# A DiT block on one core: attention output in one block per unit, and beats dealt anew

## The chip, the cores and the metric

The kernel runs on one core of a Trainium2 chip. The time is the device time of one execution in microseconds, the median of several executions. A profiled execution gives, beside its own time, the span from the first to the last instruction and what each engine did in it: TensorE (PE for matmuls, PEld for weight loads), VectorE (DVE), ScalarE (ACT), GpSimd (POOL) and SyncE (SP), which issues nearly all DMAs.

## The reference

A PixArt-style transformer block over 16 sequences of 256 tokens of width 256, in 16 heads of 16, in fp32:

```python
c_proj = silu(c) @ W_mod + b_mod                  # six vectors per sequence
q, k, v = split((ln(x) * (1 + scale_a) + shift_a) @ W_qkv + b_qkv)
x = x + gate_a * (softmax(q k^T * 16**-0.5) v @ W_proj + b_proj)
q_c = ln(x) @ W_qc + b_qc;  k_c, v_c = split(ln(context) @ W_kvc + b_kvc)
x = x + softmax(q_c k_c^T * 16**-0.5) v_c @ W_cproj + b_cproj
x = x + gate_m * (gelu((ln(x) * (1 + scale_m) + shift_m) @ W_mlp1 + b_mlp1) @ W_mlp2 + b_mlp2)
```

## The kernel before

**Units.** The work is cut into 32 attention units: a self-attention unit s and a cross-attention unit c for each of the 16 sequences, in the order s0 to s4, then s5 c0 s6 c1 and so on to s15 c10, then c11 to c15 (line 785 on). A set-up ahead of them splits the first weights and makes the first queries and keys; after them comes the MLP, four chunks of the hidden layer for each sequence, whose first pieces are worked in the last units.

**Precision.** A product of two fp32 operands is three passes in fp32r: each operand is cut in a high and a low part (`cut`, `high`, `low`), and high x high, high x low and low x high are added in PSUM.

**Softmax.** For each unit, scores S are first made with queries in rows, only for the row maxima: `s_tile` (line 691) does two matmuls into `s` and one VectorE `tensor_reduce` into `mx`. The maxima are transposed (`m_halves`, `psm`), negated by ScalarE (`m_send`, line 728) and sent by DMA into a spare row of the queries. Then the scores are made again with keys in rows, now less the maximum: `t_part` (line 734) writes `st`. One ScalarE activation, `exp` (line 745), takes both halves of `st` (one for each half of the array) to a `pt` tile: pair k of heads. `st` and `s` have one buffer each in PSUM. `av_part` (line 768) multiplies `pt` with V, which has a column of ones for the sums, into `o`; its matmuls use four groups of 32 columns of the array, where nearly all others use two groups of 64 rows. ScalarE copies `o` to `oT`; it is transposed (A0, A1 in the plan), divided by the sums on VectorE (`norm`, n0, n1), transposed back (`aT`, word a), cut, and projected (P). `end` copies the projection out of PSUM, `add` gates and adds it to x (line 657).

**Beats.** Each unit has eight beats (`beat`, line 1080). In beat k of unit n run: the scores t of pair k of unit n, the maxima's scores s of unit n+1, the projections Q and V of unit n+2 and K of unit n+3, the transposes T and U of normalized context or x for n+3, and the output of units n-1 and n-2. What runs where is written out by hand in `PLAN` (line 1068): each beat has words done ahead, words of an x lane, words of a y lane, and words done after. The lanes are the two row halves of the array: x does rows 0 to 63, y rows 64 to 127; `beside` (line 475) issues from the lane that is behind, counting one for a matmul and 0.53 for a small transpose. "Q12" is twelve matmuls of Q; s and t are two matmuls each. A y-lane piece that continues an accumulation, or the second half of a transpose, has to wait for the end of its x-lane piece (`after`, line 335). The whole plan of before stands as the removed lines at the end of the diff below: one line a beat, and in it the words ahead, the x lane, the y lane, and the words after.

E is the exponential of the beat. o0 is the attention output of pairs 0 to 3 of the unit itself, after beat 4; o1 that of pairs 4 to 7 of the unit before, after beat 0. kh and kl make the high and low part of K (ScalarE, VectorE), qh and ql those of Q; kH, kL, qH, qL send them by DMA. pe is `end`. Te, Ue, ae are ScalarE copies of transposes out of PSUM, Tc, Uc, ac their cuts on GpSimd. Words c, s, e, L are pieces of layer norms (sums on VectorE, the rest on GpSimd, or ScalarE for those called late).

**Order.** Every engine, and SP, runs its instructions in the order in which this program issues them (`InOrder`, line 40, and `ON`). So a wait at the head of an engine's queue holds all behind it.

**Buffers.** PSUM has two banks for `st`, two for `s`, and rings of two for the tags `gen` (Q, V, K, P in the order of their first matmul) and `tr` (transposes, maxima, `o`). In SBUF, `pt` has 5 buffers, `x` 5, `c` (context) 2, `t1` 2, `x1` 7.

**Last stage.** `TW` in `E_` (line 55) says after which beat the MLP's weights are loaded (u), their high parts made (h) and their low parts (l; d means VectorE, else GpSimd).

Of the kernel before, what the change touches and what calls it, by code (L numbers as in the profile page):

```python
# [10 lines left out]
F32 = mybir.dt.float32  # L11
F32R = mybir.dt.float32r
# [9 lines left out]
def pixart_block(  # L22
# [32 lines left out]
    E_ = {'M': (7, 9, 13, 15), 'CUT': 8, 'LN': {'s': 'pool', 'c': 'pool', 'q': 'pool'}, 'ON': (1, 1, 1), 'L0': -16, 'L1': 1, 'S0': -7, 'A0': 0, 'T0': 1, 'S1': 5, 'A1': 7, 'L2': 9, 'T1': 9, 'S2': 32, 'AP': 23, 'DV': (0, 1), 'HP': (1, 0), 'BZ': {}, 'AV': {1: [(1, 2), (1, 3)], 9: [(0, 0), (0, 1)]}, 'AHEAD': (0, 0, 0, 0, 0, 2), 'TW': {(21, 6): 'cb', (23, 6): 'u1', (25, 1): 'u0', (25, 7): 'u2', (27, 1): 'u3', (27, 4): 'h2p', (27, 5): 'h3p', (28, 0): 'l2d', (28, 3): 'u5 h1p', (28, 4): 'h0p', (29, 0): 'l3', (29, 1): 'l0', (29, 3): 'l1d', (29, 6): 'u7', (29, 7): 'u4 u6 h4p', (30, 1): 'h5p h6d', (30, 7): 'l6', (31, 0): 'h7p', (31, 1): 'l4', (31, 2): 'l5', (31, 6): 'l7'}, 'XP': 1, 'IL': 1, 'MF': 0, 'SH': 4, 'RAMP': 1, 'HA': 1, 'MP': 16, 'W': (7, 1, 0, 0), 'PRE': 'z0qp z0kp load rest ld2 one0 silu b12 brow L0a turn L0b b4 L0d scale T0t sc1 hik lok L1a T0h L1b T0l b4 shift hiq K0a L1d bk loq K0m K0h K0x0 K0x1 K0y0p K0y1p T1t K0l T1h K0l0 K0l1 bq T1l Q0a Q0m Q0h Q0x0 Q0y0p Q0x1 Q0y1p Q0l Q0l0 Q0l1 z1kp z1qp K1a K1b hiv lov Q1a Q1b K1x0 K1x1 K1y0 K1y1 K1l K1l0 K1l1 Q1x0 Q1x1 Q1y0 Q1y1 Q1l Q1l0 Q1l1 L2a L2b L2c V0a V0b bv b9 ld3', 'SL': {(-1, 0): 'V1a', (-1, 1): 'T2t T2h T2p vone z2kp z2qp', (-1, 2): 'V1b', (-1, 3): 'rest wm', (-1, 4): 'M0 rest one1 ld4', (-1, 5): 'K2a L3a', (-1, 6): 'K2m L3b L3p L3c', (-1, 7): 'mods sc2 one2 rest', (0, 0): 'gm rest', (0, 1): 'rest', (0, 4): 'rest', (0, 6): 'rest', (1, 0): 'rest', (1, 5): 'rest'}}  # L55
# [35 lines left out]
    ones = const.tile([8, N], F32, name="ones")  # L91
# [18 lines left out]
    def stage(w_ap, c0, name, tag="pt", bufs=5, t=None, q=SP):  # L110
# [49 lines left out]
    ts = [work.tile([P, 2, KC, H], F32, tag="pt", name=f"wf{i}", bufs=5) for i in range(3)]  # L160
# [3 lines left out]
    def f_load():  # L164
        X[0] = work.tile([P, NT, H], F32, tag="x", name="x_0", bufs=5)
# [45 lines left out]
    def setup_rest():  # L211
        gb = work.tile([B, 2, 2, H], F32, tag="pt", name="gb", bufs=5)
        gA, bb = gb[:, 0], gb[:, 1]
        bc = const.tile([1, H], F32, name="bc")
# [25 lines left out]
        wkc, wqc = stage(W_kvc, 0, "wkc_f", "g", 3), stage(W_qc, 0, "wqc_f", "c", 2)  # L240
# [242 lines left out]
    def to_stack(W, src, bias, dst, which, name):  # L483
# [51 lines left out]
        o.high, o.low = high, low  # L535
# [28 lines left out]
    def load(u):  # L564
        if u.kind == "s":
            load_x(u.b)
        elif u.kind == "m":
            mlp_load(u.b)
        else:
            u.ct = work.tile([P, NT, H], F32, tag="c", name=f"c_{u.b}")  # L570
            SP.dma_start(u.ct, tok(ctxt, u.b))
# [28 lines left out]
    def build_post(u):  # L600
# [51 lines left out]
        def end():  # L652
            t1 = work.tile([P, NT, H], F32, tag="t1", name=f"t1_{name}")
            o.t1 = t1
            ACT.copy(t1.rearrange("p t h -> p (t h)"), o.ps)

        def add():
            t1 = o.t1
            if u.kind == "s":
                POOL.tensor_tensor(t1, t1, bc_t(G[b][:, 0]), ALU.mult)  # L660
                X1[b] = o.xg
                POOL.tensor_tensor(X1[b], o.xg, t1, ALU.add)
            else:
                POOL.tensor_tensor(t1, t1, X1[b], ALU.add)
                o.out = t1
# [5 lines left out]
        def finish():  # L671
            o.out = work.tile([P, NT, H], F32, tag="t1", name=f"t1_{name}")
# [72 lines left out]
    def exp(u, pair, st):  # L745
        u.pt[pair] = work.tile([P, 2, NT, N], F32, tag="pt", name=f"pt_{u.n}_{pair}", bufs=5)
# [56 lines left out]
    def mlp_load(b):  # L803
# [3 lines left out]
        m.xt = work.tile([P, NT, H], F32, tag="x" if b > 1 else "c", name=f"x2_{b}", bufs=5 if b > 1 else 2)  # L807
# [55 lines left out]
    def to_hidden(b, c, src, park):  # L863
# [12 lines left out]
        o.high = o.keep = keep  # L876
        o.low = o.send_high = o.send_low = lambda: None
# [11 lines left out]
    def mlp_gelu(b, c):  # L889
        ph = M[b].h.pop(c)  # L890
        homes = (("pt", 5), ("qkh", 3), ("qkl", 3))
        if b == 0 and c:
            homes = (("x1", 7),) + (homes[1:] if c < 3 else (("xTh", 5), ("xTl", 5)))
# [12 lines left out]
    def mlp_second(b, c):  # L906
# [7 lines left out]
        if c == NCH - 1:  # L914
            t1 = work.tile([P, NT, H], F32, tag="t1", name=f"mt_{b}")
# [11 lines left out]
    def tail_word(w):  # L927
# [5 lines left out]
        if c == "u":  # L933
            if j < 4:
                wf[j] = stage(W_mlp1, j * H, f"w1_{j}", "x")
            else:
                wf[j] = work.tile([P, 2, H], F32, tag="x", name=f"w2_{j}", bufs=5)
# [116 lines left out]
    def visit(n, k, home=sp):  # L1054
# [25 lines left out]
    def beat(n, k):  # L1080
# [14 lines left out]
        ls = q4 if q4 and q4.kind in ("s", "m") and q4.ln else None  # L1095
        lx = q3 if q3 and q3.kind == "c" else None
        late = lx and lx.b in (0, B - 2, B - 1)
        early = lc if lc and lc.b not in (0, B - 2, B - 1) else None
# [3 lines left out]
        def attention(v, hf):  # L1102
# [7 lines left out]
            "E": exps, "o1": lambda: attention(prev, 1), "o0": lambda: attention(cur, 0),  # L1110
            "kh": on(q2, lambda: q2.K.high()), "kl": on(q2, lambda: q2.K.low()),
            "kH": on(q2, lambda: q2.K.send_high()), "kL": on(q2, lambda: q2.K.send_low()),
            "qh": on(q2 and hasattr(q2, "Q"), lambda: q2.Q.high()), "ql": on(q2 and hasattr(q2, "Q"), lambda: q2.Q.low()),
# [6 lines left out]
            "n1": on(p1, lambda: p1.norm(1)), "n0": lambda: cur.post.norm(0),  # L1120
            "pe": on(p2, lambda: p2.end()), "hadd": on(p2 and (p2.n == nu - 3), lambda: (p2.add(), p2.store())),
            "add": on(p3, lambda: p3.add()), "gate": on(p1, lambda: p1.gate()),
            "store": on(p3, lambda: p3.store()), "begin": lambda: cur.post.begin(),
            "ld": on(ls and n > 0, lambda: load(ls)),
            "lc": on(c5 and c5.kind == "c", lambda: load(c5)),
            "c1": on(lc, lambda: lc.ln[0].steps[0]()),
            "c2": on(lc or ls and ls.kind == "m", lambda: [f() for f in lc.ln[0].steps[1:]] if lc else mlp_bias(ls.b)),
            "s1": on(ls, lambda: ls.ln[0].steps[0]()),
            "s6": on(ls, lambda: ls.ln[0].steps[1]()),
            "s7": on(ls, lambda: ls.ln[0].steps[2]()),  # L1130
            "e5": on(early, lambda: early.ln[1].steps[0]()),
            "e6": on(early, lambda: [f() for f in early.ln[1].steps[1:]]),
# [7 lines left out]
            "A1": on(p1, lambda: p1.halves(1)), "A0": lambda: cur.post.halves(0),  # L1140
# [149 lines left out]
```

## Time and profile before

| | us |
|---|---|
| median of 3 runs | 747.91 (747.2 to 749.27) |
| the profiled execution's own time | 746.75 |
| its span, first to last instruction | 745.0 |
| the 32 units, from about 33 us on | some 525 |
| the MLP behind them, from about 558 us | some 187 |

In the views below, a group of instructions is named out<-in by the program's names: `mx<-s` is the reduction of the scores for the maxima, `pt<-st` the exponential. In a list in order of time, the first two columns are the start and the length in us, and xN is a run of N instructions merged; in a list of groups, the last columns are busy us, the mean of one in ns, and idle time of the engine ahead of them with what ended it.

### The profile page before, as it was taken

The numbers are of one execution on the slowest core, as the hardware profiler recorded it, in microseconds if no ns is written. First come the engines' busy times: TensorE is split into PE (matmuls) and PEld (weight loads), VectorE is DVE, ScalarE is ACT, GpSimd is POOL, SyncE is SP. The second block draws the span as 40 slices with busy tenths as digits, with TensorE's granted clock in tenths as the row PEclk, the third lists the DMA queues.
The fourth block names the chain that finished last, engine by engine and source line by source line (L and its number), as shares of the span: only waits on it lengthen the run. The fifth ranks groups of instructions, "written<-read, shape, count | busy, mean of one in ns | idle before, by whom it ended". The sixth has DMA issues, their size and how long they took to land.

```text
span 745.0 us, 25353 instructions
## 1 busy us (share of the span) xinstructions
PE 734.8 (99%) x10144; PEld 648.7 (87%) x10144; DVE 578.8 (78%) x1190; ACT 564.2 (76%) x978; POOL 490.1 (66%) x610
## 2 busy tenths in 40 slices
PE   9999999999999999999999999999999999999997
PEld 8778888888888888888888888878878999999997
DVE  4888898988888888888889888898726656666662
ACT  4278888888888888888888888888895666666663
POOL 6756676857667485765758678667566666666553
PEclk9999999999999999999999999999999999999999
DMA  6755445443644544454444545544213132221211
GB/s 207 200 147 153 133 126 143 123 130 100 171 120 128 146 117 145 109 165 128 136 142 123 158 129 160 153 115 126 70 59 100 49 80 70 61 85 43 85 45 43
DMA packets 78809, 87.98 MB, mean 118 GB/s; under 512 B 8610, under 2 KB 64196, under 8 KB 78692
## 3 DMA queue, kind: packets, MB, share of 16 engines
q1 hardware_dynamic: 78356, 85.58, 40.4%
q8 instruction: 80, 1.31, 0.8%
q0 software_dynamic: 192, 0.52, 0.3%
q10 hardware_dynamic: 144, 0.26, 0.2%
q14 instruction: 37, 0.30, 0.1%
HBM read 26.97 MB, written 8.46 MB: 48 GB/s over the span
## 4 chain that ended last, share of the span: by engine, by line
PE 95%; DVE 2%; issue 1%; POOL 1%; ACT 1%; POOLq 0%; DVEq 0%; ACTq 0%
PE s L51 18%; PE st L51 16%; PE o L51 16%; PE ph L51 11%; PE ps_qc L51 5%; PE ps_q L51 4%; PE ps_kc L51 3%; PE ps_P_s L51 3%; PE ps_v_s L51 3%; PE ps_v_c L51 3%; PE ps_k L51 3%; PE ps_P_c L51 2%; PE ps_h L51 1%; PE psT_q L51 1%; PE psA_c L51 1%; PE psT_m L51 1%
## 5 line engine op out<-in xcount | busy, mean ns | idle before, releaser
L51 DVE TENSOR_REDUCE mx<-s 128x2 f32<-128x512 f32 x504 | 324.8, 684 | 63.1 <-PE s L51 56.5
L51 ACT ACTIVATE pt<-st 128x1024 f32<-128x1024 f32 x252 | 258.8, 1027 | 17.7 <-PE st L51 11.7
L51 PE MATMUL s<-big 63*128 63x256 f32 (+1 forms) x1024 | 184.6, 298 | 0.5 <-DVE mx L51 0.4
L51 PEld LDWEIGHTS s<-big 63*128 63x128 f32 (+1 forms) x1024 | 133.8, 186 | 19.9 <-DVE l_kc L51 6.6
L51 PE MATMUL st<-big 64*128 64x256 f32 (+1 forms) x1024 | 134.3, 298 | 0.3 <-ACT pt L51 0.2
L51 POOL TENSOR_TENSOR hl<-hf,hh 128x512 fp32r<-128x512 f32 x64 | 84.0, 1315 | 66.2 <-ACT hh L51 66.2
L51 PE MATMUL o<-pt,v 128*32 128x256 f32 x2048 | 123.8, 382 | 0.0
L51 PEld LDWEIGHTS st<-big 64*128 64x128 f32 (+1 forms) x1024 | 96.1, 185 | 16.2 <-issue 12.9
L51 PEld LDWEIGHTS o<-pt,v 128*32 128x32 f32 x2048 | 60.0, 109 | 41.4
L51 ACT ACTIVATE hf<-ph,bT 128x256 f32<-128x256 f32 x114 | 47.8, 472 | 26.8 <-PE ph L51 26.8
L51 ACT ACTIVATE hh<-ph,bT 128x256 fp32r<-128x256 f32 x114 | 47.8, 471 | 24.2 <-PE st L51 12.8
L51 ACT COPY oT<-o 128x512 f32<-128x512 f32 x63 | 36.9, 585 | 32.8 <-PE o L51 32.8
L51 DVE TENSOR_SCALAR xn_m<-x,mv_m,rs_m 128x256 f32<-128x256 f32 x28 | 26.1, 973 | 38.0 <-POOL rs_m L51 38.0
L51 PE MATMUL s<-big,hh 128*128 128x256 f32 x256 | 46.8, 282 | 0.0
L51 PE MATMUL st<-big,hh 128*128 128x256 f32 x256 | 46.5, 281 | 0.0
L51 PE MATMUL ph<-wkch,wself 128*128 128x256 f32 x224 | 45.0, 284 | 0.0
L51 PE MATMUL ph<-wqch,wself 128*128 128x256 f32 x224 | 44.9, 284 | 0.0
L51 PE MATMUL ps_k<-xTh_s,wself 64*128 64x256 f32 (+1 forms) x232 | 43.8, 294 | 0.0
L51 PE MATMUL ps_q<-xTh_s,wself 64*128 64x256 f32 (+1 forms) x240 | 39.7, 283 | 0.4 <-DVE l_q L51 0.4
L51 PE MATMUL ps_v_s<-wself,xTh_s 64*128 64x256 f32 x224 | 39.2, 294 | 0.0
L51 PE MATMUL ps_P_s<-wself,xTh_as 64*128 64x256 f32 x256 | 39.0, 282 | 0.0
L51 PEld LDWEIGHTS st<-big,hh 128*128 128x128 f32 x256 | 39.0, 188 | 0.0
(245 smaller groups left out, 2469.2 us busy)
## 6 DMA issues: line engine op xcount, KB each, us to landing
big<-h_kc SPq DMA_DIRECT2D x64, 128.0 KB
big<-h_qc SPq DMA_DIRECT2D x64, 128.0 KB
big<-h_k SPq DMA_DIRECT2D x62, 128.0 KB
big<-h_q SPq DMA_DIRECT2D x62, 128.0 KB
big<-l_k SPq DMA_DIRECT2D x32, 128.0 KB
big<-l_q SPq DMA_DIRECT2D x32, 128.0 KB
g<-gd SPq DMA_DIRECT2D x16, 256.0 KB
c<-in_ctx_dram SPq DMA_DIRECT2D x16, 256.0 KB
```

Source lines behind the costliest of these rows:

```text
L51: i = f(*a, **k)
```

## The change

- Both halves of the attention output, o0 and o1, now run for the unit before, one right after the other after beat 0; `E` stands between them on ScalarE. For that `pt` gets 8 buffers. The last unit still does its first half itself (words oz, Az, nz).
- To make room: `x` has 3 buffers and holds the context too (tag `c` is gone), `t1` has one; x is not kept for the residual but loaded a second time, in `begin`, into the `x1` tile where `gate` adds to it. Loads of unit n+5 (`lc`) are all in beat 5. The MLP's inputs go to `xTh` and `xTl`, some weights to `g`, `pt` and `x`, and `TW` is dealt anew, with every cut on GpSimd.
- `end` is VectorE's, not ScalarE's: it multiplies the projection by the gate (s) or adds x (c) on its way out of PSUM; GpSimd's `add` is left with one addition for s, none for c.
- Queries: ScalarE takes both rows blocks out of PSUM with the bias in fp32 (`rows`), and GpSimd makes the high part and the low part (`cut`); before, ScalarE made the high part and VectorE the low part.
- The plan of beats is new. Only the cross units of the first and the last sequence do the layer norm of x late (before: the first and the last two).

```diff
+        def rows():
+            o.hi = work.tile([P, KC, N], F32R, tag="qkh", name=f"h_{name}", bufs=3)
+            o.lo = work.tile([P, KC, N], F32R, tag="qkl", name=f"l_{name}", bufs=3)
+            for f in range(KC):
+                ACT.activation(o.lo[:, f].bitcast(F32), o.ps[:, f * N:(f + 1) * N], AF.Identity, bias=bias[f])
+
+        def cut():
+            POOL.tensor_copy(o.hi, o.lo.bitcast(F32))
+            POOL.tensor_tensor(o.lo, o.lo.bitcast(F32), o.hi, ALU.subtract)
...
+            o.xg = work.tile([P, NT, H], F32, tag="x1", name=f"xg_{b}", bufs=7)
+            SP.dma_start(o.xg, tok(x, b))
 
         def gate():
             if u.kind == "c":
                 return
-            o.xg = work.tile([P, NT, H], F32, tag="x1", name=f"xg_{b}", bufs=7)
-            POOL.tensor_tensor(o.xg, X[b], bc_t(G[b][:, 1]), ALU.add)
+            POOL.tensor_tensor(o.xg, o.xg, bc_t(G[b][:, 1]), ALU.add)
...
         def end():
-            t1 = work.tile([P, NT, H], F32, tag="t1", name=f"t1_{name}")
-            o.t1 = t1
-            ACT.copy(t1.rearrange("p t h -> p (t h)"), o.ps)
+            t1 = work.tile([P, NT, H], F32, tag="t1", name=f"t1_{name}", bufs=1)
+            o.t1 = o.out = t1
+            ps = o.ps.rearrange("p (t h) -> p t h", t=NT)
+            if u.kind == "s":
+                DVE.tensor_tensor(t1, ps, bc_t(G[b][:, 0]), ALU.mult)
+            else:
+                DVE.tensor_tensor(t1, ps, X1[b], ALU.add)
 
         def add():
-            t1 = o.t1
             if u.kind == "s":
-                POOL.tensor_tensor(t1, t1, bc_t(G[b][:, 0]), ALU.mult)
                 X1[b] = o.xg
-                POOL.tensor_tensor(X1[b], o.xg, t1, ALU.add)
-            else:
-                POOL.tensor_tensor(t1, t1, X1[b], ALU.add)
-                o.out = t1
+                POOL.tensor_tensor(X1[b], o.xg, o.t1, ALU.add)
...
-        u.pt[pair] = work.tile([P, 2, NT, N], F32, tag="pt", name=f"pt_{u.n}_{pair}", bufs=5)
+        u.pt[pair] = work.tile([P, 2, NT, N], F32, tag="pt", name=f"pt_{u.n}_{pair}", bufs=8)
...
     PLAN = [
-        ("kh", "s t m1", "m1 t s", "m1s kH E o1 add gate kl"),
-        ("c1", "s t Q12", "t P2 s P10", "L1 ld kL E"),
-        ("", "s t T pe A1 V3", "s t Q4 T A1 Q1", "hadd E L2 Te Tc c2"),
-        ("", "s t V9", "Q1 t s Q6", "E n1"),
-        ("qh store", "s t", "s t qH", "E L3 o0 ql qL"),
-        ("", "t s a E m0 K6", "t s V4 a m0 V2", "ae ac m0s e5 lc s1"),
-        ("", "s t K1 A0 K5 U E", "V2 t s V4 U A0", "begin e6 Vk Ue s6"),
-        ("", "s t P12", "K2 t s K1 K9", "E n0 Uc s7"),
+        ("", "s t m1", "m1 t s", "m1s kh o0 E o1 kH gate kl c1 c2 e5 e6 s1 s2 kL"),
+        ("", "s t A0 Q6 T Q2", "t P4 s A0 n0 P4 T", "E L1 Te Tc c3"),
+        ("", "s t A1 Q4 V4", "P4 pe s t A1 n1 Q4", "E L2 add store m2 e7"),
+        ("", "s t V8", "Q8 qh s t", "E qc qH qL s3"),
+        ("", "s t a K4", "t s V4 a", "E L3 ae ac"),
+        ("", "s t m0 K6", "V6 s t m0", "E m0s oz lc m5"),
+        ("", "s K2 t U Vk P4", "V2 s t K4 U", "begin E Ue Uc m6"),
+        ("", "Az s t P8", "K2 t s Az K6", "E nz m7"),
     ]
```

qh is now `rows`, qc the new `cut`; A0 and n0 now stand for the unit before, as A1 and n1 do.

More of the change, by code (lines that the diff above doesn't have):

```diff
@@ L90, in pixart_block @@
     wself = const.tile([P, 16, H], F32R, name="wself")
-    ones = const.tile([8, N], F32, name="ones")
+    ones = work.tile([8, N], F32, tag="oT", name="ones")
     DVE.memset(ones, 1.0)
@@ L104, in load_x, with stage @@
     def load_x(b):
-        X[b] = work.tile([P, NT, H], F32, tag="x", name=f"x_{b}", bufs=5)
+        X[b] = work.tile([P, NT, H], F32, tag="x", name=f"x_{b}", bufs=3)
         SP.dma_start(X[b], tok(x, b))
     brow = const.tile([32, P], F32, name="brow")
-    def stage(w_ap, c0, name, tag="pt", bufs=5, t=None, q=SP):
+    def stage(w_ap, c0, name, tag="pt", bufs=8, t=None, q=SP):
         if t is None:
@@ L158, in busy @@
             PE.matmul(where[:, :P], wz, wz, start=True, stop=True)
-    ts = [work.tile([P, 2, KC, H], F32, tag="pt", name=f"wf{i}", bufs=5) for i in range(3)]
+    ts = [work.tile([P, 2, KC, H], F32, tag="pt", name=f"wf{i}", bufs=8) for i in range(3)]
     wm0, wm1, wk, wq, wv = (ts[i // 2][:, i % 2] for i in range(5))
@@ L164, in f_load @@
     def f_load():
-        X[0] = work.tile([P, NT, H], F32, tag="x", name="x_0", bufs=5)
+        X[0] = work.tile([P, NT, H], F32, tag="x", name="x_0", bufs=3)
         ACT.dma_start(X[0], tok(x, 0))
@@ L671, in finish @@
         def finish():
-            o.out = work.tile([P, NT, H], F32, tag="t1", name=f"t1_{name}")
+            o.out = work.tile([P, NT, H], F32, tag="t1", name=f"t1_{name}", bufs=1)
             DVE.tensor_tensor(o.out.rearrange("p t h -> p (t h)"), o.ps,
@@ L874, in keep @@
             M[b].kept.append(c)
-        o.high = o.keep = keep
-        o.low = o.send_high = o.send_low = lambda: None
+        o.high = o.keep = o.rows = keep
+        o.low = o.cut = o.send_high = o.send_low = lambda: None
         return o
@@ L933, in tail_word @@
         if c == "u":
+            home = ("g", 3) if j in (3, 7) else ("x", 3)
             if j < 4:
-                wf[j] = stage(W_mlp1, j * H, f"w1_{j}", "x")
+                wf[j] = stage(W_mlp1, j * H, f"w1_{j}", *home)
             else:
-                wf[j] = work.tile([P, 2, H], F32, tag="x", name=f"w2_{j}", bufs=5)
+                wf[j] = work.tile([P, 2, H], F32, tag=home[0], name=f"w2_{j}", bufs=home[1])
                 SP.dma_start(wf[j], W_mlp2[(j - 4) * H:(j - 3) * H].rearrange("(k p) c -> p k c", p=P))
@@ L1094, in beat @@
         lc = q4 if q4 and q4.kind == "c" else None
-        ls = q4 if q4 and q4.kind in ("s", "m") and q4.ln else None
+        ls = q4 if q4 and q4.kind == "s" else None
         lx = q3 if q3 and q3.kind == "c" else None
-        late = lx and lx.b in (0, B - 2, B - 1)
-        early = lc if lc and lc.b not in (0, B - 2, B - 1) else None
+        late = lx and lx.b in (0, B - 1)
+        early = lc if lc and lc.b not in (0, B - 1) else None
+        lm = q4 if q4 and q4.kind == "m" and q4.ln else None
         c5 = unit(n + 5)
@@ L1109, in beat @@
         do = {
-            "E": exps, "o1": lambda: attention(prev, 1), "o0": lambda: attention(cur, 0),
+            "E": exps, "o0": lambda: attention(prev, 0), "o1": lambda: attention(prev, 1),
+            "oz": lambda: attention(cur if cur.n == nu - 1 else None, 0),
             "kh": on(q2, lambda: q2.K.high()), "kl": on(q2, lambda: q2.K.low()),
             "kH": on(q2, lambda: q2.K.send_high()), "kL": on(q2, lambda: q2.K.send_low()),
-            "qh": on(q2 and hasattr(q2, "Q"), lambda: q2.Q.high()), "ql": on(q2 and hasattr(q2, "Q"), lambda: q2.Q.low()),
+            "qh": on(q2 and hasattr(q2, "Q"), lambda: q2.Q.rows()), "qc": on(q2 and hasattr(q2, "Q"), lambda: q2.Q.cut()),
             "qH": on(q2 and hasattr(q2, "Q"), lambda: q2.Q.send_high()), "qL": on(q2 and hasattr(q2, "Q"), lambda: q2.Q.send_low()),
```

49 lines of the change are left out of this document (28 added, 21 removed).

## The prediction

> **What bounds the kernel now.** I read the page first, then busy time by stretches, groups by shape, TensorE's and ScalarE's instructions in order of time, and TensorE's waits. The page, and two stretches of one unit each:
>
> ```profile
> span 745.0 us, 25353 instructions
> ...
> PE 734.8 (99%) x10144; PEld 648.7 (87%) x10144; DVE 578.8 (78%) x1190; ACT 564.2 (76%) x978; POOL 490.1 (66%) x610
> ```
>
> ```profile
> 303.50:319.60 16.10, 16.10 (x264) 13.60 (x264) 13.71 (x29) 13.27 (x21) 9.82 (x16) 1.00 0.43 114
> 319.60:335.70 16.10, 16.10 (x269) 13.78 (x268) 14.34 (x33) 13.91 (x23) 11.47 (x15) 1.00 0.54 153
> ```
>
> Columns: the stretch and its length; busy us of PE, PEld, DVE, ACT, POOL; granted clock; DMA share; GB/s. A unit takes 16.1 us and TensorE is busy in all of it; the other engines have 1.8 us or more to spare. TensorE's program order shows how it spends a unit. One beat with two lanes of matmuls, and the start of the next:
>
> ```profile
> 317.24 0.27 PE L51 MATMUL ps_q<-xTh_s,wself 64*128 64x256 f32 x1
> 317.39 0.51 PE L51 MATMUL st<-big 64*128 64x256 f32 x4
> 317.73 0.28 PE L51 MATMUL s<-big 63*128 63x256 f32 x1
> ...
> 318.10 0.28 PE L51 MATMUL ps_q<-xTh_s,wself 64*128 64x256 f32 x1
> ...
> 318.57 0.28 PE L51 MATMUL ps_q<-xTl_s,wself 64*128 64x256 f32 x1
> ...
> 318.81 0.61 PE L51 MATMUL s<-big 63*128 63x256 f32 x4
> 319.14 0.51 PE L51 MATMUL st<-big 64*128 64x256 f32 x4
> ```
>
> The y lane's ps_q starts at 318.10, 318.22, 318.33, 318.45, 318.57: one **slot** is 0.118 us, and a second matmul runs beside it in the other lane. Four st matmuls take 0.51 after an interruption and 0.43 without one (315.78, below): each restart costs 0.10. ScalarE around the same time:
>
> ```profile
> 315.83 0.59 ACT L51 COPY t_s<-ps_P_s 128x512 f32<-128x512 f32 x1 [0.47 <-PE ps_P_s L51]
> 316.31 1.03 ACT L51 ACTIVATE pt<-st 128x1024 f32<-128x1024 f32 x1
> 317.22 0.59 ACT L51 COPY y_c<-psT_c 128x512 f32<-128x512 f32 x1
> 318.00 1.02 ACT L51 ACTIVATE pt<-st 128x1024 f32<-128x1024 f32 x1 [0.18 <-PE st L51]
> 318.92 0.83 ACT L51 ACTIVATE h_q<-ps_q,bqkv 128x256 fp32r<-128x256 f32 x2
> ```
>
> ```profile
> 315.78 0.43 PE L51 MATMUL st<-big 64*128 64x256 f32 x4
> ```
>
> This is the loop to watch. The two halves of st are one buffer; one exponential reads both, so no score matmul t of beat k+1 may start before the exponential of beat k has ended. It ended at 317.34, and st started at 317.39, 0.05 later, although TensorE had come to it after 317.24. Then four st matmuls (last start 0.23 after the first), and the exponential at 318.00, 0.10 after the last of them ended at 317.90. So from the **last** t start of a beat to the **first** t of the next there must pass 0.28 + 0.10 + 1.03 + 0.05 = 1.46 us, or 12.4 slots. In the order of before both lanes have t in their first four slots of every beat, and beats are 12 to 16 slots or hold an attention block, so the loop just fits; that is the 1.0 us step of this kernel that its beats hide.
>
> **The change, part by part.**
>
> *Attention output in one block.* Its matmuls run four abreast in another shape:
>
> ```profile
> 311.48 0.28 PE L51 MATMUL s<-big 63*128 63x256 f32 x1
> ...
> 313.55 0.38 PE L51 MATMUL s<-big 63*128 63x256 f32 x1
> ...
> 313.77 0.28 PE L51 MATMUL s<-big 63*128 63x256 f32 x1
> ```
>
> ```profile
> 303.52 1.93 PE L51 MATMUL o<-pt,v 128*32 128x256 f32 x32
> ```
>
> Eight groups of four take 1.93 with the last one's 0.38 in it: 0.22 a group. From 311.48 to 313.55 are 2.07; less one slot, plus the restart (0.22 instead of 0.12 to 313.77), a block costs 2.05, of which 0.29 are going in and out. One block of sixteen groups costs 3.81 instead of 2 x 2.05: **-0.29 a unit**. Eight buffers let all eight exponentials of a unit wait for it; the first exponential of the next unit comes after the block's first half and hides under the second.
>
> *Beats dealt anew.* Counting slots of the longer lane (transposes half a slot), beats 0 to 7 had 4.5, 16, 13.2, 13, 4, 12.6, 12.1, 16 and get 4.5, 16.2, 14.2, 12, 10.1, 10.5, 10, 12 (beat 6 is 2.1 longer in every other unit): 92.5 becomes 90.6 in the mean, **-0.22 us**. So TensorE's own work is 90.6 x 0.118 + 3.81 = 14.5 us. Before it was 10.9 + 4.1 = 15.0, so its 16.1 hold 1.1 of small waits.
>
> The new places of t are what I see against it. In the x lane t is at slots 2 to 4 (in beat 6 at 4 to 6), in the y lane: beat 2 at 6 to 8, beat 3 at 10 to 12, beat 4 at 0 to 2, beat 5 at 8 to 10, beat 6 at 4 to 6, beat 7 at 2 to 4, beat 0 at 0.5 to 2.5. TensorE issues in program order, so a waiting t holds both lanes. Rows used below:
>
> ```profile
> L51 DVE TENSOR_REDUCE mx<-s 128x2 f32<-128x512 f32 x504 | 324.8, 684 | 63.1 <-PE s L51 56.5 <-PE psm L51 0.8
> L51 ACT ACTIVATE m<-psm 16x128 fp32r<-16x128 f32 x64 | 17.0, 265 | 5.7 <-issue 3.2 <-PE psm L51 1.5 <-ACT h_kc L51 0.2
> L51 ACT COPY v<-ps_v_s 128x512 f32<-128x512 f32 x14 | 8.1, 579 | 0.0
> L51 DVE TENSOR_TENSOR t_c<-psP_c,xg 128x512 f32<-128x512 f32 x2 | 1.4, 677 | 0.0
> ```
>
> - Beat 4: the last t of beat 3 starts at slot 11. Ahead of its exponential ScalarE now has the query rows (0.83, on Q's last matmul at slot 7): 7 x 0.118 + 0.38 + 0.83 = 2.04, then 1.03 + 0.05: t may start at 3.12 after beat 3's start, and TensorE is there at 1.42. Wait 1.7.
> - Beat 5: y's two t and then x's two follow the wait, the last starting 0.46 after the first; 0.46 + 1.46 = 1.92, and TensorE is there after 0.10 + 11 slots = 1.4. Wait 0.5.
> - Beat 6: y's last t is 7 slots after x's first: 0.10 + 0.83 + 1.46 = 2.4; TensorE has 12.5 slots, 1.6. Wait 0.8. Then projection P must wait in the same beat for V's buffer: ScalarE does m (0.27) and the V copy (0.58) behind that late exponential. Wait 0.4 (0.5 or 0.25 by unit).
> - Beat 7: 0.2. Beat 0: 12 slots are 1.42 against 0.23 + 1.46: 0.3.
> - Beat 2: V takes the buffer of P, which VectorE's new gate frees. P's last matmul starts at slot 3 (0.35 + 0.38 = 0.73), a reduction is ahead (to about 1.1), the gate takes 0.68: 1.8 against V at 10.1 slots = 1.2. Wait 0.6.
> - Beat 1: T's y half follows its x half at once. The same pairing in before:
>
> ```profile
> 324.59 0.22 PE L51 MATMUL psT_q<-ident,xn_q 64*128 64x64 f32 x1
> 324.65 0.22 PE L51 MATMUL psA_s<-ident,oT 64*128 64x64 f32 x1
> 324.88 0.27 PE L51 MATMUL psT_q<-ident,xn_q 64*128 64x64 f32 x1
> ```
>
> 0.23 from 324.65 to 324.88. Wait 0.2.
>
> Waits 1.7 + 0.5 + 0.8 + 0.4 + 0.2 + 0.3 + 0.6 + 0.2 = 4.7, and seven restarts 0.7, less 0.2 because ScalarE's neighbours overlap (two of 0.47 took 0.83): 5.2. A unit: 14.5 + 5.2 = **19.7 us, +3.6**. The old small waits (U's half, K behind K at beats 6 to 7, t of beat 3) go; I add none in their place.
>
> *VectorE gates, GpSimd splits queries.*
>
> ```profile
> L51 DVE SCALAR_TENSOR_TENSOR l_q<-ps_q,bqkv,h_q 128x256 fp32r<-128x256 f32 x32 | 13.9, 476 | 1.7 <-ACT h_q L51 1.7
> L51 POOL TENSOR_TENSOR t_s<-t_s,g 128x512 f32<-128x512 f32 x16 | 20.9, 1307 | 0.0
> L51 POOL CAST xTh_c<-y_c 128x512 fp32r<-128x512 f32 x16 | 9.8, 611 | 43.0 <-ACT y_c L51 43.0
> ```
>
> VectorE -2 x 0.48 + 0.68 = -0.3 a unit, ScalarE -0.59, GpSimd -1.31 + 0.61 + 1.3 = +0.6: 11 to 12 of 19.7 us. None becomes a bound; queries are sent at beat 3's end and read in the next unit's beat 0, behind five beats.
>
> *x loaded twice, other homes.* 16 more loads of 256 KB, 4 MB beside 88, at 0.43 to 0.54 DMA share. They stand on SP in beat 6 behind the maxima's send and ahead of the next unit's, each needing an x1 buffer freed over a unit before; only unit 1's may wait, for a weight split on GpSimd (2 us once). Context and x come in at beat 5 and are read in the next beat 0, two beats or 3 us and more later. t1's one buffer is read out in the beat it is written in, a unit ahead of its next use. All that at nothing; if SP or GpSimd were late, up to 1 us a unit. Weights of the last stage are split wholly on GpSimd in units 28 to 30, 3.8 us a unit: covered by the longer unit. One context unit more has its x normalized on GpSimd and not ScalarE: nothing either way.
>
> **Sum.** 28 units x 3.6 = 101. Units 28 to 30 took 17.2 in the mean:
>
> ```profile
> 481.00:498.30 17.30, 16.98 (x271) 14.05 (x271) 15.32 (x31) 14.83 (x24) 12.50 (x18) 1.00 0.52 149
> 498.30:515.90 17.60, 16.76 (x273) 13.97 (x275) 15.05 (x30) 15.01 (x25) 14.30 (x18) 1.00 0.43 121
> 515.90:532.50 16.60, 16.58 (x262) 13.91 (x260) 14.42 (x29) 13.46 (x22) 10.08 (x14) 1.00 0.39 116
> ```
>
> +2.5 each, 7.5. Unit 31 has a second bank for t and no maxima: 0. Units 0 and 1 lack P: -2. Last stage unchanged. Together +106 on this execution's 746.75 (span 745.0; the median is 747.91): **853**. Bounds: without the rows ahead of the exponential, the V waits and T's half, 18.0 a unit, 806; with the 0.6 that my tally leaves unexplained in before again, 20.5, 878.
>
> **Rivals.**
>
> *Faster: the loop is hidden.* If t never waits, the unit gains 0.29 + 0.22 + about 0.3 of old small waits, less 0.2: -0.6 x 31, 728. For it: TensorE's weight loads waited for exponentials only twice in the main stage, and ScalarE has 2 to 3 us a unit free. Against: 317.34 and 317.39. It decides from the point where st's last t and next first t lie over 12.4 slots apart; in beats 3 to 4 they lie one apart. Chance 0.08.
>
> *Slower by half.* Waits overlap better than I add them (one long wait lets ScalarE and VectorE catch up, so the V and P waits vanish, and beats 5 to 7 shrink): 17 to 18 a unit, 770 to 806. Chance 0.12.
>
> *Slower still: the clock, or a second loop.* Granted clock was 1.00 even at 17.60 us with 16.76 busy, but a unit with a quarter of idle time isn't in this trace. At half clock the distances between t in beats 3 to 7 grow by some 20 slots, 2.4 us a unit: 920. [...] With late GpSimd or SP, 878 and up. Chance 0.12.
>
> *No change*: savings equal waits, 0.02.
>
> **Numbers.** The loop as summed has 0.66. From 800 to 885 lie that case and some of its neighbours, 8 in 10. About 0.3% is what a measurement of this kernel can tell from no change; faster by more 0.08, within 0.02, slower 0.90.
>
> **What would show it.** Stretches of one unit near 19.7 us with PE idle or st waiting for pt; In beat 4, some 1.7 us without TensorE, with the two rows of Q ahead of the exponential on ScalarE and st 0.05 after its end; the same, shorter, in beats 5 and 6; ps_v right after VectorE's t_s; one o block of x64 in 3.7 us where two of x32 stood (if it still falls in two, 0.29 is lost again). Wrong: a unit at 15.5 with t not waiting; or a clock below 1.00.

## The result: 866.72 us, and the profile after

| | before | after |
|---|---|---|
| median of 4 runs each, us | 748.07 (747.2 to 749.27) | 866.72 (863.8 to 870.41) |
| ratio, 95% interval | | 1.1587 [1.1538, 1.1636] |
| profiled execution: own time, span, us | 746.75, 745.0 | 870.41, 868.6 |

The changed kernel is 119 us slower in the median; the profiled execution lies 124 above that of before. Ratios are taken over the fast runs; of all runs below one counts as slow, `old_plan`'s at 849.37 us, and without it that kernel's median is 840.01, 3 less than in its table. Of the page after, the busy times, the granted clock, the chain of work that ended last and two groups of instructions:

```profile
span 868.6 us, 25137 instructions
...
PE 793.3 (91%) x10144; PEld 675.5 (78%) x10144; DVE 588.6 (68%) x1156; ACT 552.8 (64%) x946; POOL 510.0 (59%) x646
...
PEclk8999999999999999999999999999889999999999
...
PE 77%; ACT 10%; POOL 3%; DMA 3%; DVE 3%; issue 2%; SPq 1%; POOLq 0%; ACTq 0%
...
L51 PE MATMUL st<-big 64*128 64x256 f32 (+1 forms) x1024 | 175.9, 307 | 48.0 <-ACT pt L51 42.1
L51 PEld LDWEIGHTS st<-big 64*128 64x128 f32 (+1 forms) x1024 | 121.9, 188 | 72.8 <-ACT pt L51 63.7
```

The chain and the same two groups before:

```profile
PE 95%; DVE 2%; issue 1%; POOL 1%; ACT 1%; POOLq 0%; DVEq 0%; ACTq 0%
...
L51 PE MATMUL st<-big 64*128 64x256 f32 (+1 forms) x1024 | 134.3, 298 | 0.3 <-ACT pt L51 0.2
...
L51 PEld LDWEIGHTS st<-big 64*128 64x128 f32 (+1 forms) x1024 | 96.1, 185 | 16.2 <-issue 12.9
```

TensorE, 99% busy before, is idle for 9% of the span, and ScalarE has 10% of the chain where it had 1%. The waits of TensorE's weight loads and matmuls for `pt` (the exponentials) were the loop of the prediction: 63.7 and 42.1 us, where the matmuls had waited 0.2 us in all. The waits of TensorE's matmuls, longest first (in total, times, longest):

```profile
PE st L51 <- ACT pt L51: 42.1, 37, 1.3
PE s L51 <- DVE mx L51: 5.6, 4, 2.7
PE st L51 <- DMA big<-m: 3.6, 7, 1.4
PE s L51 <- DMA big<-l_qc: 2.9, 3, 1.9
```

Two units of the changed kernel, then two near the end; each stretch runs from one block of the attention output to the next:

```profile
315.46:334.88 19.42, 17.64 (x262) 14.20 (x260) 14.96 (x32) 13.13 (x20) 11.56 (x18) 1.00 0.43 123
334.88:354.33 19.45, 17.87 (x271) 14.56 (x269) 14.11 (x28) 13.40 (x20) 10.80 (x14) 1.00 0.42 114
...
572.51:595.19 22.68, 19.76 (x270) 15.29 (x269) 14.19 (x28) 13.42 (x20) 11.00 (x14) 0.92 0.42 117
595.19:619.34 24.15, 19.59 (x270) 16.09 (x268) 15.39 (x33) 14.27 (x22) 14.41 (x20) 0.88 0.36 102
```

A unit of 16.1 us became 19.4. From the first steady block (53.68 us in before, 59.25 after) the difference of 123.7 us between the spans (744.97 and 868.62) is: 5.6 up to that block; 26 units of 16.13 now at 19.74 in the mean (eight of them take over 20), 93.8; units 27 to 30, 23.2 together; unit 31, 2.3; the last stage -1.2. And this is beat 4's wait, in ScalarE's and TensorE's program order (in brackets the engine's idle time before the instruction, and what ended it):

```profile
344.86 0.47 ACT L51 ACTIVATE l_q<-ps_q,bqkv 128x256 f32<-128x256 f32 x1
345.22 1.02 ACT L51 ACTIVATE pt<-st 128x1024 f32<-128x1024 f32 x1
```

```profile
346.29 0.38 PE L51 MATMUL st<-big 64*128 64x256 f32 x1 [1.26 <-ACT pt L51]
```

The rows of the query, then the exponential, which ends at 346.24, and 0.05 later st. TensorE's previous matmul had started at 344.76; a slot of 0.118 later it could have gone on, so the wait is 1.42.

### The profile page after: what moved, and what is told of

The parts are those of the page before. It is cut to its first block, busy times and chain, and to the rows that moved or that the text cites. A ratio compares the mean times of both kernels' runs of the same rounds, so it can differ in the third digit from the quotient of the medians.

```text
span 868.6 us, 25137 instructions
## 1 busy us (share of the span) xinstructions
PE 793.3 (91%) x10144; PEld 675.5 (78%) x10144; DVE 588.6 (68%) x1156; ACT 552.8 (64%) x946; POOL 510.0 (59%) x646
## 3 DMA queue, kind: packets, MB, share of 16 engines
q8 instruction: 80, 1.31, 0.7%
## 4 chain that ended last, share of the span: by engine, by line
PE 77%; ACT 10%; POOL 3%; DMA 3%; DVE 3%; issue 2%; SPq 1%; POOLq 0%; ACTq 0%
PE o L51 14%; PE st L51 13%; PE s L51 12%; PE ph L51 9%; ACT pt L51 5%; PE ps_qc L51 4%; PE ps_q L51 4%; PE ps_P_s L51 3%; PE ps_P_c L51 3%; PE ps_kc L51 2%; PE ps_v_c L51 2%; DVE mx L51 2%; DMA big<-m 2%; PE ps_v_s L51 2%; PE ps_k L51 1%
## 5 line engine op out<-in xcount | busy, mean ns | idle before, releaser
L51 DVE TENSOR_REDUCE mx<-s 128x2 f32<-128x512 f32 x504 | 338.0, 687 | 153.9 <-PE s L51 146.8
L51 ACT ACTIVATE pt<-st 128x1024 f32<-128x1024 f32 x252 | 258.5, 1026 | 70.8 <-PE st L51 65.1
L51 PE MATMUL s<-big 63*128 63x256 f32 (+1 forms) x1024 | 225.1, 296 | 12.4 <-DVE mx L51 5.6
L51 PE MATMUL st<-big 64*128 64x256 f32 (+1 forms) x1024 | 175.9, 307 | 48.0 <-ACT pt L51 42.1
L51 PEld LDWEIGHTS s<-big 63*128 63x128 f32 (+1 forms) x1024 | 159.5, 188 | 35.6 <-DVE mx L51 17.8
L51 PEld LDWEIGHTS st<-big 64*128 64x128 f32 (+1 forms) x1024 | 121.9, 188 | 72.8 <-ACT pt L51 63.7
L51 PEld LDWEIGHTS o<-pt,v 128*32 128x32 f32 x2048 | 63.9, 111 | 44.7 <-issue 3.1
L51 ACT ACTIVATE hh<-ph,bT 128x256 fp32r<-128x256 f32 x114 | 47.8, 471 | 24.2 <-PE st L51 12.8
L51 DVE TENSOR_SCALAR xn_m<-x,mv_m,rs_m 128x256 f32<-128x256 f32 x28 | 24.1, 904 | 36.4 <-POOL rs_m L51 36.4
L51 POOL TENSOR_TENSOR xg<-xg,g 128x512 f32<-128x512 f32 x16 | 20.5, 1284 | 46.1 <-DMA xg<-in_x_dram 46.1
L51 ACT ACTIVATE m<-psm 16x128 fp32r<-16x128 f32 x64 | 16.6, 259 | 48.5 <-PE s L51 46.0
L51 PE MATMUL ps_P_s<-wself,xTh_as 64*128 64x256 f32 x256 | 43.2, 288 | 2.4 <-ACT v L51 2.4
L51 PE MATMUL ps_q<-xTh_s,wself 64*128 64x256 f32 (+1 forms) x240 | 44.3, 309 | 1.0 <-DVE l_q L51 0.2
```

The lines of the kernel that those rows point to most:

```text
L51: i = f(*a, **k)
```

## The experiments

The theory at first: the places of t against the exponentials' loop are the cause. Its rivals: the two splits of work (GpSimd cuts the queries, VectorE gates), the joined block, the transfers. Before, run beside each group, had medians of 747.4 to 748.1 us.

**The order of t and of the rows in the new beats.**

```diff
 beat 3 of the changed kernel: x "s t V8", y and then:
-"Q8 qh s t", "E qc qH qL s3"
+"Q8 s t",    "E qh qc qH qL s3"     rows_behind
+"s t Q8",    "E qh qc qH qL s3"     t_first_3
```

> The changed kernel, with ScalarE's two rows of Q behind the exponential of beat 3 and not ahead of it. The loop of t and the exponential: the exponential starts 0.3 us sooner, so the wait of t in beat 4, 1.42 us in the changed kernel's profile, falls to about 1.1; 0.3 x 31 = 9 us, 857. If GpSimd's lateness counts, its cut starts 0.7 us later and the time is the same or up to 5 us more.

Measured: 880.13 us (877.91 to 882.35), ratio 1.1776 [1.1735, 1.1816]. That is 13 us more than the changed kernel, above both branches. The gap between matmul starts at beat 4's t fell from 1.54 to 1.31 us only. The st matmuls' waits for `pt` fell by 6 us in all, from 42.1 to 36.4, and those for the maxima and for their transfers rose by 8 (mx 5.6 to 9.5, `big<-m` 3.6 to 7.3). These two sums explain 2 of the 13 us; the rest stays open.

> As the one with the rows behind, and in beat 3 the y lane's s and t ahead of Q. The last t of beat 3 starts at slot 3 and not 11, the next first t at slot 12: 9 slots of the 12.4 have passed, and the wait of t in beat 4 is 0.4 us, not 1.42: 1.0 to 1.2 us a unit less, 830 to 836. If the waits only move (what t no longer waits for in beat 4 is waited for in beats 5 to 7), the gain is under 0.5 a unit, over 850.

Measured: 867.8 us (867.23 to 868.37), ratio 1.1611 [1.1587, 1.1634]. The step on t worked as expected, its gap in beat 4 fell to 0.43, and the time stayed. The rival had the number right, but not the place: the waits that came instead are not those of t in beats 5 to 7.

```profile
PE s L51 <- DVE mx L51: 9.6, 11, 3.0
PE s L51 <- DMA big<-l_qc: 8.7, 9, 1.7
PE st L51 <- DMA big<-m: 8.6, 16, 2.2
PE st L51 <- ACT pt L51: 7.3, 25, 1.6
```

The scores now wait for the queries' low part and, behind it on SP, for the maxima. This run also makes the queries later by itself, since Q comes behind t and its rows behind the exponential; so it doesn't tell the lost cover from the later start. A unit without such a wait took 18.44 us (335.77 to 354.21). The mean clock is 0.975, in the changed kernel 0.985: of what t gave back, part can have gone there, at most 9 us as an estimate (0.010 of 865).

**t moved in the kernel before**, to find what its place is worth by itself:

```diff
 beat 3 of before, y:
-"Q1 t s Q6"
+"Q1 s Q6 t"
```

> The kernel before with one edit: in beat 3 the y lane does its t at the end (slots 9 to 11) and not at slots 1 to 3. The matmuls are the same. By the loop, beat 4's first t comes 5 slots after the last t of beat 3 where 12.4 must pass: 7.4 slots and a restart, 0.9 to 1.0 us a unit, 776 to 780. If TensorE can cover it (ScalarE has 2 to 3 us a unit free), the time stays within 3 us of before.

Measured: 769.61 us (769.39 to 769.83), ratio 1.0297 [1.0276, 1.0317]. One t, moved behind s and six matmuls of Q, costs 22 us where 29 to 33 were expected; a unit takes 16.92 us in the mean instead of 16.13. The loop is shown, in a kernel in which nothing else was changed; TensorE's waits there, once a unit:

```profile
PE st L51 <- ACT pt L51: 16.8, 32, 0.6
```

**The beats of before with the rest of the change.** `old_plan` has the two blocks and, word for word as far as they have a place, the beats of before:

```diff
-("", "s t m1", "m1 t s", "m1s kh o0 E o1 kH gate kl c1 c2 e5 e6 s1 s2 kL"),
...
+("kh", "s t m1", "m1 t s", "m1s kH E o1 gate kl"),
+("c1", "s t Q12", "t P2 s P10", "L1 kL E m2"),
+("", "s t T pe A1 V3", "s t Q4 T A1 Q1", "E L2 add Te Tc c2 c3 m4"),
+("", "s t V9", "Q1 t s Q6", "E n1"),
+("qh store", "s t", "s t", "E L3 o0 qc qH qL"),
+("", "t s a E m0 K6", "t s V4 a m0 V2", "ae ac m0s e5 lc s1 m5"),
+("", "s t K1 A0 K5 U E", "V2 t s V4 U A0", "begin e6 e7 Vk Ue s2 m6"),
+("", "s t P12", "K2 t s K1 K9", "E n0 Uc s3 m7"),
```

> The changed kernel with all its other parts (eight buffers, x loaded twice, VectorE's gate, GpSimd's split of the queries, the new homes) but the beats and the two attention blocks of before. If the places of t in the beats made the loss, a unit is back at 16.0 to 16.3 us and the time at 745 to 756. If the moved engine work, the second load or late GpSimd and SP made it, the unit stays over 17.5 us and the time over 790.

Measured: 842.82 us (836.71 to 849.37), ratio 1.1217 [1.1184, 1.125]. The first theory fell: with t where it was, 95 us of 119 stayed. One thing is not as in the changed kernel: the queries come out of PSUM in beat 4 and are cut behind that beat's layer norm, where the changed kernel does both in and right after beat 3. So what the cut costs below, it costs in this place. The next three runs undid the splits in this kernel, one at a time and both:

```diff
 old_q: ScalarE and VectorE split the queries; beat 4 as in before
-("qh store", "s t", "s t", "E L3 o0 qc qH qL"),
+("qh store", "s t", "s t qH", "E L3 o0 qc qL"),
-"qh": q2.Q.rows(), "qc": q2.Q.cut()
+"qh": q2.Q.high(), "qc": q2.Q.low()
 old_gate: ScalarE copies the projection, GpSimd gates and adds
-DVE.tensor_tensor(t1, ps, bc_t(G[b][:, 0]), ALU.mult)
+ACT.copy(t1.rearrange("p t h -> p (t h)"), o.ps)
+POOL.tensor_tensor(t1, t1, bc_t(G[b][:, 0]), ALU.mult)
```

> The changed kernel with the beats and the two blocks of before, and with the queries split by ScalarE and VectorE as before; VectorE still gates the projection. With the queries cut by GpSimd this kernel took 842.8 us, and its profile gave about 31 us of TensorE's waits to the queries' DMAs (l_qc 16.7, the maxima behind them 7.1, 3.4 of issue, l_q 2.3, h_qc 1.2) and 33 to V behind VectorE's gate. Theory (two costs that add): the first 31 go and some of what hangs on them, 800 to 815 us. Rival 1 (the queries are the whole cause, V's wait lies beside them): 745 to 765. Rival 2 (the gate is the whole cause): over 830.

> The changed kernel with the beats and the two blocks of before, and with the projection copied out by ScalarE and gated and added by GpSimd as before; GpSimd still cuts the queries. Theory (two costs that add): V's 33 us of waits go and some of what hangs on them, 800 to 815 us. Rival 1 (the queries are the whole cause): over 830, since GpSimd gets two more operations of its own. Rival 2 (the gate is the whole cause): 745 to 765.

> The changed kernel with the beats and the two blocks of before and both splits of work undone: what is left of the change is the eight buffers of exponentials with the other tensors' new homes, x loaded a second time and the MLP's due times. Theory (these cost nothing): 745 to 758 us. Rival (transfers of x or fewer buffers of x cost half a microsecond a unit or more): over 765.

| beats and blocks of before, and | us (range) | over before, 95% |
|---|---|---|
| both splits new (`old_plan`) | 842.82 (836.71 to 849.37) | 1.1217 [1.1184, 1.125] |
| VectorE gates (`old_q`) | 785.1 (784.75 to 785.45) | 1.0493 [1.0472, 1.0514] |
| GpSimd cuts the queries (`old_gate`) | 825.87 (821.18 to 830.57) | 1.1037 [1.0963, 1.1112] |
| neither (`old_both`) | 745.52 (744.73 to 745.98) | 0.9964 [0.9949, 0.9978] |

Both of the two middle numbers missed 800 to 815, one below and one above: the gate alone costs 40 us, the queries alone 80, both 97. `old_both` hit: with both splits undone, eight buffers, x loaded twice, the new homes and the MLP's due times cost nothing, and this kernel beats before by 0.4%. Of that, 1.2 us show in the profiles, in the last stage.

The gate, in `old_q`, in the half of a unit that holds V, and VectorE's program order in it:

```profile
280.29:289.62 9.33, 8.02 (x130) 6.64 (x128) 7.73 (x18) 6.69 (x11) 4.95 (x7) 1.00 0.47 143
```

```profile
284.58 1.29 DVE L51 TENSOR_REDUCE mx<-s 128x2 f32<-128x512 f32 x2 [0.58 <-PE s L51]
285.79 0.68 DVE L51 TENSOR_TENSOR t_c<-ps_P_c,xg 128x512 f32<-128x512 f32 x1
286.38 0.24 DVE L51 BATCH_NORM_AGGREGATE mv_c<-st_c 128x2 f32<-128x6 f32 x2
```

The half takes 9.33 us, in `old_both` 7.91. TensorE's V products start at 286.62 after a gap of 1.50: the gate stands behind two reductions on VectorE, and V takes the bank which the gate reads. In 16 of 28 such cases, 19.6 us, the profile names the statistics' `mv_c` as what ended the wait, because that came last. But V's weight load starts at 286.58, after the gate's end at 286.47 and ahead of `mv_c`'s at 286.62, and with the gate undone no wait of that kind is left: it is the gate that holds the bank.

The queries, in `old_gate`, from GpSimd's cut over SP's queue to the scores. The block at the end of beat 4 begins at 228.66 here, and ScalarE has the rows ready at 228.76:

```profile
230.59 1.09 POOL L51 TENSOR_SCALAR xn_c<-c,less_c,rs_c 128x256 f32<-128x256 f32 x2
231.63 0.61 POOL L51 CAST h_qc<-l_qc 128x512 fp32r<-128x512 f32 x1
232.33 1.29 POOL L51 TENSOR_TENSOR l_qc<-l_qc,h_qc 128x512 fp32r<-128x512 f32 x1
```

```profile
232.27 2.48 SPq L51 DMA_DIRECT2D big<-h_qc  x4
234.86 1.19 SPq L51 DMA_DIRECT2D big<-l_qc  x2
236.14 0.54 SPq L51 DMA_DIRECT2D big<-m  x1
```

The cut starts 2.9 us after that, behind a cut of x and the pieces of a layer norm in GpSimd's order. It takes 1.9, SP's issues of six transfers 3.7 from the first half of the cut on, and TensorE's first s that reads the queries starts at 237.57, 1.50 after its predecessor. In `old_both` the first of these transfers is issued 0.25 us ahead of the same block (207.14 against 207.39), here 3.6 behind it: the queries are 3.9 us later, and the maxima's transfer stands behind them on SP. In its waits:

```profile
PE s L51 <- DMA big<-l_qc: 17.4, 12, 2.3
PE st L51 <- DMA big<-m: 7.3, 17, 2.2
PE s L51 <- DMA big<-l_q: 6.0, 5, 2.2
```

These are 31 us of the 80. The clock can have a share in the rest: its mean is 0.969 in `old_gate` and 0.998 in `old_both`. If it fell to 0.50, as in the changed kernel (the last section), about 6% of 819 us ran so and up to 25 us were lost, an estimate; by it at least 24 us of the 80 are not accounted for.

**The splits undone in the new beats.** The second theory: loop and splits stand side by side in the changed kernel and hide one another.

> The changed kernel with one block per unit, t ahead of the queries' products in beat 3 and the queries split by ScalarE and VectorE as before. With the cut on GpSimd this order took 867.8 us, and its profile gave about 22 us to the queries' DMAs and the maxima behind them, while its units without such a wait took 18.4 us. Theory (t's wait and the late queries lie side by side, so that the first shows only once the second is gone): all units near 18.4, 2.3 over before, so 60 more than before's 748, and 15 to 25 for the last units: 822 to 835 us. Rival (the order of beat 3 is worth nothing, the waits go elsewhere in the plan): over 850.

> The changed kernel, its beats and its one block per unit, with both splits of work undone: the queries split by ScalarE and VectorE, the projection copied out by ScalarE and gated and added by GpSimd. With the beats of before this undoing was worth 97 us. Theory (the exponentials' loop and the two splits hide one another, so that the loop keeps what it costs when the splits go): 838 to 858 us, since in the profile of the changed kernel only about 0.3 us a unit stood behind the queries' DMAs and 0.3 behind the gate. Rival (the splits are the cause here too, the dealing of the beats is nearly free): 765 to 790 us.

> The changed kernel with t ahead of the queries' products in beat 3 and both splits of work undone. With only the queries' split undone this took 847.1 us, 19.07 from block to block, with gaps of 0.33 before V's products behind VectorE's gate and 0.92 before the keys' in beat 5 behind VectorE's second cut of the queries. Theory (VectorE's gate costs here too, itself and by what it makes late): 18.0 to 18.8 from block to block, 820 to 840 us. Rival (the gate is hidden once a unit has one block): 845 to 850.

| new beats, one block, and | us (range) | over before, 95% |
|---|---|---|
| as changed | 866.72 (863.8 to 870.41) | 1.1587 [1.1538, 1.1636] |
| both splits undone (`after_both`) | 855.31 (854.37 to 856.26) | 1.1419 [1.1344, 1.1494] |
| t first in beat 3, queries undone (`t_first_q`) | 847.11 (845.95 to 848.27) | 1.1321 [1.1296, 1.1347] |
| t first in beat 3, both undone (`t_first_both`) | 847.11 (845.75 to 848.47) | 1.1309 [1.1233, 1.1386] |

`after_both` hit: undoing both splits, worth 97 us in the old beats, is worth 11 here. Its unit:

```profile
329.43:348.67 19.24, 17.68 (x270) 14.44 (x268) 14.43 (x29) 13.81 (x21) 10.26 (x13) 1.00 0.43 112
```

```profile
PEld st L51 <- ACT pt L51: 65.1, 115, 1.5
```

With both splits undone the unit still takes 19.24, 1.41 of it beat 4's wait, and the weight loads wait as long for `pt` as in the changed kernel. `t_first_q` took 21 us off `t_first_3`, half of what was expected, and lies between its two branches (the clock, 0.991 against 0.975, can be up to 14 us of it, 0.016 of 845, an estimate), with units of 19.08: t now waits 0.3 in beat 4, but beat 5's keys wait for the bank of the queries, which VectorE's low parts release late.

```profile
PE ps_kc L51 <- DVE l_q L51: 7.1, 11, 0.7
PE st L51 <- ACT pt L51: 5.8, 23, 0.9
PE ps_k L51 <- POOL xn_q L51: 5.3, 8, 0.7
```

Undoing the gate as well gave nothing (847.11 again), as the rival in `t_first_both` had it. The gap of 0.33 that its expectation puts down to V is another: it lies between the last transpose and the second part of Q (349.28 to 349.61 in `t_first_q`), which waits for the end of Q's first part, and it stays at 0.33 with the gate undone (350.58 to 350.91). V itself starts 0.05 after the gate's end (349.83 and 349.78) and loses 0.1. The gap before the keys stayed too, 0.92 to 0.94 and then 0.98 to 1.00. So each remedy uncovered the next wait.

**One block, in the beats of before.** From `old_both`, only the first half of the attention output moves, and in beat 6 U goes ahead of K1:

```diff
-("kh", "s t m1", "m1 t s", "m1s kH E o1 gate kl"),
-("c1", "s t Q12", "t P2 s P10", "L1 kL E m2"),
+("kh", "s t m1", "m1 t s", "m1s kH o0 E o1 gate kl"),
+("c1", "s t A0 Q12", "t P2 s A0 n0 P10", "L1 kL E m2"),
...
-("qh store", "s t", "s t qH", "E L3 o0 qc qL"),
+("qh store", "s t", "s t qH", "E L3 qc qL"),
...
-("", "s t K1 A0 K5 U E", "V2 t s V4 U A0", "begin e6 e7 Vk Ue s2 m6"),
+("", "s t U K1 Az K5 E", "V2 t s V4 U Az", "begin e6 e7 Vk Ue s2 m6"),
```

> The beats of before with both splits as before (745.5 us so far, two blocks a unit), and of the new dealing the one block alone: the first half of the attention output goes from the end of beat 4 to the block at the end of the next unit's beat 0, its halves and division to beat 1. In beat 6 U's x half comes ahead of K, since the halves left that place. Theory (the block was what the exponentials' loop ran beside): beat 5 opens with t, so it waits the loop of 1.46 us less a slot, 1.35, against 0.29 saved by one block fewer; 1.06 a unit, 770 to 780 us. Rival 1 (one block is a saving, it is the new order of the beats that costs): 735 to 742. Rival 2 (what one block moves sets off further waits, so that it is most of the 110 us between the two dealings): over 800.

Measured: 802.57 us (801.68 to 803.46), ratio 1.073 [1.0688, 1.0772]. That is 57 us over `old_both`, above the theory's range and over 800 as the second rival had it, though it is half of the 110 us between the two dealings and not most. A unit, and the waits for the exponential:

```profile
341.66:359.26 17.60, 16.39 (x271) 14.06 (x269) 13.57 (x29) 13.71 (x22) 8.63 (x12) 1.00 0.44 119
```

```profile
PE st L51 <- ACT pt L51: 37.3, 33, 2.5
```

The wait at beat 5's t is a gap of 1.386 between starts in each unit, 1.27 without the slot, where 1.35 was expected. Then s waits 0.44 for the maxima in every other unit, 0.1 is lost at each of three or four more restarts, and units 27 and 28 take 20.3 and 20.5. So the mechanism stands, and with what it sets off the block costs twice what was expected. The other half, the new dealing with two blocks, was not run.

**The last units.** In the changed kernel the MLP's statistics on VectorE stand in front of the maxima and wait for GpSimd's bias.

```diff
-"E L3 ae ac"         m5: bias and statistics
+"E L3 ae ac m4"      m4: bias; m5: statistics
```

> The changed kernel with the MLP's bias (GpSimd) ahead of its statistics (VectorE) by a beat, in the last five units alone. Theory (the statistics wait for GpSimd in front of the maxima, 2.3 and 2.7 us of TensorE's wait for the maxima in units 28 and 29, and less in 27 and 30): 859 to 863 us, 4 to 8 less than the changed kernel. Rival (the MLP's transfers and bias are late by themselves): 865 to 868.

Measured: 863.44 us (861.63 to 867.43), ratio 1.1519 [1.146, 1.1579]: not to be told from the changed kernel's 863.8 to 870.41. The reason is in GpSimd's queue and VectorE's:

```profile
609.95 1.29 POOL L51 TENSOR_TENSOR xTl_ac<-y_ac,xTh_ac 128x512 fp32r<-128x512 f32 x1
611.19 1.27 POOL L51 TENSOR_TENSOR x<-x,cb 128x512 f32<-128x512 f32 x1
```

```profile
612.49 0.75 DVE L51 BATCH_NORM_STATS2 st_m<-x 128x6 f32<-128x256 f32 x2 [3.70 <-POOL x L51]
```

The bias comes right behind the cut of the attention output in both kernels, since nothing stands between beats 4 and 5 on GpSimd; VectorE waits the same 3.70 in both. Before had the bias in beat 2. Putting it there wasn't tried, so the wait is shown and its price isn't.

## Why the prediction came out right, and where its steps did not

**Direction and mechanism: right.** st started 0.05 us after the exponential, ScalarE had the rows of the query ahead of it, beat 4 was the longest wait of a steady unit. The new beats and the one block without either split cost 110 us against `old_both` (855.31 and 745.52): 57 when the block comes first, 53 more for the dealing. Predicted for them and the rest together: 106.

**The sum: 3.6 predicted, 3.3 in the two units below and 3.6 in the mean, and that is luck: both of its terms were off.** I take the gaps of 0.2 us and more between matmul starts, each less a slot, and leave going into and out of a block to the block, as the prediction does. Then two units hold 1.12 us of such gaps in before (271.28 to 303.52) and 7.53 after (334.88 to 373.75):

| one unit, us | predicted | measured |
|---|---|---|
| TensorE's own work, before and after | 15.0, 14.5 | 15.56, 15.67 |
| waits and restarts, before and after | 1.1, 5.2 | 0.56, 3.77 |

The waits grew by 3.2 and not by 4.1, and the savings of 0.5 didn't come: the slots of the longer lane (92.5 to 90.6) don't give the time of the new beats. Why the own work didn't shrink was not settled. The waits, one by one: beat 4 1.42 (predicted 1.7), beat 5 0.1 (0.5), beat 6 0.5 (0.8; half of it is s behind VectorE's reduction, not t), V copy 0.36 in every other unit (0.4), beat 7 0.14 (0.2), beat 0 0.1 (0.3), V behind the gate 0.1 (0.6), T 0.2 (0.2). One more of 0.2, Q's second part behind its first in beat 2, wasn't in the sum. The small ones are smaller, as the second rival had it ("one long wait lets ScalarE and VectorE catch up"), but not the big one.

**GpSimd, SP and the queries at nothing: nearly right in the changed kernel, and for a reason not given.** I set the cut of the queries behind "five beats" of cover; between the end of beat 3 and the next beat 0 they are four. In the new beats undoing both splits gives 11 us, 0.4 a unit, within "if SP or GpSimd were late, up to 1 us a unit". In the beats of before the same two cost 97, with the cut in a later place. The cover was in good part the wait in beat 4. In the changed kernel SP has issued the last of the queries' transfers 2.0 us ahead of beat 0's first s (370.71 and 372.72); in a late unit of `t_first_3`, where beat 4 waits 0.31 and not 1.42, it has done so 0.7 us ahead of where s could start (333.06 and 333.74), and s starts at 334.50. But there the queries also start later by themselves, so the share of each is not shown. The gate costs V 0.1 here, 1.4 a unit in `old_q`.

**x twice, eight buffers, homes, due times at nothing: right with both splits undone**, and a little better (`old_both`). There GpSimd waits 6.6 us in all for the second load of x. In the changed kernel it waits 46.1, up to 6.8 at a time and at the head of its queue; whether this makes the queries later was not tried.

**Units 27 to 30: +23, not about 11.** I costed weight splits there and didn't look at where the MLP's bias stands for VectorE; TensorE waits 2.6 and 3.0 us for the maxima in units 28 and 29, and the clock reads 0.50 from 613.6 and from 637.4 beside it (below). **Start: +5.6, not -2**; 6.8 us at a clock of 0.50 lie in it (12.8 to 19.6), and what made the rest is not shown. **Unit 31: +2.3, not 0.**

The first two rivals (728; 770 to 806) fell with the unit's 19.4; of the third, the clock had a small part (0.50 in 24 us of 869).

## What to carry to other kernels

The attention blocks were also the place where ScalarE's loop ran unseen (with one of two moved, `old_one_block` took 57 us more); before joining two stretches of long work, ask what each of them covers, and give that loop a new cover of at least its length (1.46 us here). A wait that is removed can uncover the next one (in `t_first_3` the gap at beat 4 fell from 1.54 to 0.43 and the time stayed), and several causes of a slow-down need not add: test each with the others undone (97 us of the splits in one order of the beats, 11 in another), and call an edit free only together with the wait that hides it. TensorE's waits for a buffer lasted until its last reader was done (st started 0.05 us after the exponential, V's weight load in `old_q` 0.11 after the gate): count what stands ahead of that reader on its engine (1.29 us of reductions ahead of the gate).

## What the runs showed of the hardware

In three stretches of the changed kernel a clock of 0.50 came beside waits of 2 to 3 us, although TensorE was busy most of the time around them (58.9 of the 70.8 us from 572.51 to 643.34):

```profile
572.60:576.00 3.40, 3.40 (x36) 1.68 (x40) 2.74 (x8) 1.11 (x3) 0.22 (x1) 0.50 0.26 65
613.60:620.40 6.80, 4.98 (x46) 4.29 (x50) 4.80 (x10) 2.05 (x5) 6.21 (x10) 0.50 0.13 37
637.40:644.30 6.90, 4.88 (x46) 4.20 (x50) 4.80 (x10) 1.76 (x4) 4.49 (x8) 0.51 0.15 39
```

The first follows a wait of 2.17 us (from 569.52) by 0.9 us. The last two start within 1 us of the beginning of waits of 2.59 and 2.96 us for the maxima (from 612.83 and 636.46) and last 6.8 and 6.9. In these two the clock fell before the wait was over. A fourth stretch, at the start (12.8 to 19.6, 0.50), has no such wait ahead of it: between 1.04 us and 12.8 TensorE's longest is 0.21. That the waits are what lowers the clock is read from the order in time in three cases and not tested. What the clock costs shows in the block of the attention output at 619.34: its groups of four matmuls start 0.43 us apart at 0.50 (619.34, 619.77, 620.19) and 0.22 apart at 1.00 (from 620.50 on). The prediction gave the clock 2.4 us a unit if it fell throughout; it fell in 24 us of 869, the stretch at the start with it, and in the last 2.5, behind TensorE's last matmul.
